# A list schedule with one key per operation in place of a table by operation names

## The chip, the cores and the metric

The kernel runs on one core of one Trainium2 chip. The metric is the device time of one execution in microseconds (us). Five engines work side by side, each on its own list of instructions, in the order in which the program was built: PE (TensorE, matmuls), DVE (VectorE), ACT (ScalarE), POOL (GpSimd) and SP (SyncE, which here only issues DMAs). An instruction that needs something from another engine waits for a semaphore, and everything behind it on its engine waits as well.

## The reference

Two batches of 2048 tokens with 512 features go through a Mamba-2 layer and a feed-forward layer with ternary weights; each is added to its input and normalised. Cut to what is computed:

```python
def reference(u, W_in, conv_w, conv_b, dt_bias, A_log, D, norm_w, W_out, W_up, W_gate, W_down):
    # mamba: 1024 inner features, 8 heads of 128, state of 64, one group
    zxbcdt = einsum('bld,ed->ble', u, W_in)
    z, xBC, dt = zxbcdt[..., :1024], zxbcdt[..., 1024:2176], softplus(zxbcdt[..., -8:] + dt_bias)
    xBC = silu(conv_b + sum(shifted(xBC, k) * conv_w[:, k] for k in range(4)))   # causal, 4 taps
    x, B, C = xBC[..., :1024], xBC[..., 1024:1088], xBC[..., 1088:]
    y = ssd(x, dt, -exp(A_log), B, C) + x * D        # scan over time, in chunks
    yg = y * silu(z)
    yn = yg * rsqrt(mean(yg * yg) + 1e-5) * norm_w
    x1 = layernorm(u + einsum('ble,de->bld', yn, W_out))
    # feed-forward: 2048 hidden features, weights rounded to -1, 0, 1 times mean(|W|)
    up, gate = einsum(x1, ternary(W_up)), einsum(x1, ternary(W_gate))
    return layernorm(x1 + einsum(silu(up) * gate, ternary(W_down)))
```

## The kernel before

**Operations and planner.** The kernel doesn't call the engines in the order of its text. It first records operations: `op(name, engine, cost, function, r=..., w=...)` (the method of class `Order`, and its short name `op` in the kernel) notes a name, an engine, a planned duration, what is read and what is written; from the reads and writes come the dependences. There are 5631 operations; one is a few instructions, a group of 8 or 12 matmuls for instance. `run` then plays a list schedule: whenever an engine is free, it takes, of the operations that are ready and find their buffers free, the one with the smallest key. The sequence in which operations are taken is the sequence in which `emit` issues them, so the keys decide the order on every engine, the DMA issues on SP included, and which of the buffers of a pool an operation gets. Buffers in SBUF and PSUM banks are given out by the planner as well.

Two more rules of `run` touch the order: an ACT operation whose function lies in another table than the last one (silu or exp) counts 12 later than its key, and its planned duration grows by 1.3.

**Keys.** `keys` goes through the operations backwards and finds for each the latest start that its due time and its successors allow; then it looks up the operation's name in `TABLE`. A name followed by `@0` is of group 0 or of FFN block 0; a name without it stands for all other groups, whose keys are the table's number plus the group's origin (46 us per mamba group, 765 + 77 us per FFN block). Operations that the table doesn't have keep the latest start, and those without any due time behind them, such as the warm-up groups, get an infinite key: they are taken when nothing else is ready.

**Stages.** The mamba stage works on 16 groups of 256 tokens (two chunks of 128). For a group, by names of operations:

- `ul` loads u, `usq`, `usmm`, `usmx`, `pw`, `rc` find a scale, `uh` (ACT) and `ulo` (DVE) split u into two f16 halves.
- `x0` to `x8` (PE, L633, 12 matmuls of 260 columns each into a bank of "mm"); `t.3` (ACT, L638) and `t.0` to `t.2` (DVE, L640) are the convolution; `xs` is its silu (ACT, L644); `xt` transposes it on PE (L648) into the bank "tr", `xe` copies it out (ACT, L650).
- `z00` to `z12` (PE, L616, 12 matmuls of 344 columns into "mm") and their silu `sz` (ACT, L623).
- `e` to `q7` are the softplus and the step sizes, `cmm` the cumulative sums (PE, L705, L706); they go through DRAM (`cst`, `cr`, `ec`), are subtracted (`sg`, DVE, L724) and go through exp (`xf`, `xg`, `xec`, ACT, L742 to L747).
- For each chunk, `gps`, `yo` (PE, L776, from the state), `st` (PE, L791) and `stu` (DVE, L798, the state's update), `m`, `md` (DVE, L806, L808), `yd` (PE, L813), `yg` (DVE, L815), then the normalisation `ssq`, `rs`, `pw`, `yh` (ACT), `yl` (DVE), two transposing DMAs `th`, `tl`, and `o0` to `o2` (PE, L833, 8 matmuls of 512 columns each into the one bank "po"), copied out by `s` (ACT, L836) and stored by `ss`.

A group's scan is recorded behind the next group's projections, so two or more groups are in work at a time. Beside them run the FFN weights' loads, means and rounding (L857, L877, L878). At the very front 80 groups of 4 matmuls on constants (L572) keep PE busy while the weights come in; they have the bank "po" and no use otherwise.

The FFN stage works on 8 blocks of 512 tokens. Each block is loaded, normalised, split and transposed (`Fs` to `FT`), then goes through 8 pairs: per pair seven products `FP1` to `FP7` (PE, L935, 8 matmuls of 256 columns, a Strassen-like scheme) in banks A, B and C, with copies of half-finished banks in between (`Fk1` to `Fk3`, ACT, L939 and L944: `Fk1` copies A after product 1 into B, and products 6, 7 and 4 go on adding to A), sums on DVE (`Fc`, L940), silu (`Fa`, ACT, L956), and `Fg`, `Fh`, `Fl`. Then 16 downs `Fd` (PE, L1015, 8 matmuls of 512 columns), 4 for each of 4 row tiles, and for each tile the sum `Fr`, the normalisation `Fe`, `Fq`, `Fy`, `Fm` and the store `Fo`.

Of the kernel before, what the change touches and what calls it, by code (L numbers as in the profile page):

```python
# [37 lines left out]
TABLE = {  # L38
    "tl.1@0": -1082.32, "Fl0.7@0": -1029.81, "Fh0.5@0": -1021.38, "Fh1.3@0": -971.19, "xt2@0": -912.02, "gm.0@0":
    -890.46, "x0@0": -869.16, "Fk1.6@0": -867.44, "xs1@0": -839.63, "x3@0": -839.01, "z00@0": -808.27, "Fd12@0":  # L40
    -786.29, "cmm@0": -776.73, "Fq0@0": -760.02, "Fh1.5@0": -752.59, "Fa1.1@0": -742.14, "Fc22.5@0": -740.59,
    "Fc12.7@0": -709.75, "FP5.6@0": -682.02, "Fd10@0": -672.67, "FP6.3@0": -670.8, "Fq3@0": -649.25, "Fc22.7@0":
    -634.31, "Fe1@0": -614.87, "Fa1.3@0": -567.75, "FP6.1@0": -563.53, "md1.1@0": -547.28, "Fd13@0": -524.72, "t33@0":
    -521.47, "FP4.5@0": -514.84, "wb7ld": -512.65, "Fu0@0": -509.75, "Fh0.1@0": -508.71, "wx8rc": -501.51, "FP6.1":
    -500.94, "Fl6@0": -497.1, "Fu1@0": -494.77, "T30": -493.63, "Fh1.4@0": -492.92, "Fp0@0": -490.89, "Fd22@0": -486.86,
    "Fa1.1": -483.51, "FS5@0": -482.63, "t71@0": -479.96, "FP5.7@0": -478.29, "FP2.2@0": -473.05, "md1.1": -463.02,
    "FP4.1@0": -461.9, "t11@0": -460.67, "yl.0@0": -460.49, "Fl0.7": -459.64, "wx3sq": -458.4, "q_5@0": -458.28,
    "Fl1.6@0": -453.42, "Fk2.1@0": -448.32, "ssq.0": -444.97, "Fh0.7@0": -444.58, "xec0@0": -443.77, "t23@0": -443.66,
    "FP6.4@0": -441.24, "Fc22.6@0": -436.89, "T10": -432.63, "Fk3.0@0": -431.18, "q2@0": -429.41, "FP7.3@0": -429.11,
    "FP7.5": -419.45, "s.1@0": -419.15, "Fs3@0": -418.15, "Fk3.4@0": -416.72, "FS4@0": -416.22, "Fk1.2@0": -408.87,  # L50
    "t70@0": -406.53, "q_11@0": -399.23, "FT5@0": -398.13, "FT0@0": -378.4, "wz1hi": -376.4, "Fk2.2@0": -375.97,
    "q_9@0": -375.64, "t72@0": -373.53, "wb0hi": -371.27, "cst0": -370.61, "t11": -370.46, "xe2@0": -370.3, "Fl0@0":
    -369.99, "t82@0": -366.39, "szs1": -362.42, "q_3@0": -361.43, "Fl1.7@0": -360.58, "Fa2.7@0": -358.67, "t12@0":
    -356.74, "q3@0": -354.24, "Fk3.6@0": -350.89, "th.0@0": -350.43, "Fk1.5@0": -344.81, "stc.0@0": -344.79, "FT4@0":
    -341.61, "xe": -340.43, "Fl0.4@0": -339.88, "nA0": -339.38, "xw0.0@0": -335.61, "Fg0.0@0": -334.33, "usq@0":
    -330.91, "xt3@0": -330.1, "t42@0": -329.77, "Fg1.3@0": -329.03, "Fs2@0": -327.97, "wz2lo": -327.63, "FP1.1@0":
    -324.63, "xf": -321.24, "FP5.6": -321.23, "Fk1.2": -319.88, "FP7.1@0": -319.05, "rs.0@0": -318.4, "xt4": -317.17,
    "m1.0@0": -315.45, "t63": -314.69, "Fc22.4@0": -314.08, "Fh0.6@0": -313.89, "Fm1@0": -312.11, "Fa1.5@0": -309.81,
    "Fr3@0": -307.28, "FP3.1": -306.64, "Fq1@0": -296.16, "xe4@0": -296.16, "Fk2.0@0": -294.21, "Fu2@0": -291.89, "t40":
    -291.26, "cs0@0": -289.33, "Fr1@0": -288.39, "cwu1": -288.17, "cst@0": -283.89, "yd1.0@0": -283.77, "Fl0.0@0":  # L60
    -282.86, "FP3.6@0": -282.73, "FP3.1@0": -282.02, "xt0@0": -281.89, "wz1mm": -281.66, "Fg1.4@0": -280.5, "FT1@0":
    -279.98, "Fa1.4@0": -279.57, "yg1.1@0": -279.25, "wz0mm": -277.61, "Fl1.4@0": -276.92, "ul@0": -276.33, "t21@0":
    -276.31, "Fo3@0": -275.9, "cr1@0": -274.67, "Fy1@0": -272.88, "v0@0": -272.69, "Fr1": -271.9, "x5@0": -271.5,
    "Fh1@0": -270.66, "md0.0": -270.5, "Fg1.7@0": -270.05, "Fa2.0@0": -269.63, "cwu2": -269.24, "ulo@0": -268.86, "q6":
    -266.76, "FP1.7@0": -266.69, "Fk2.6@0": -266.34, "FP6.5@0": -265.81, "Fl1.0@0": -262.07, "Fe2@0": -261.65, "xs5@0":
    -260.73, "t51@0": -259.32, "Fk3.0": -259.28, "q1@0": -257.63, "z12@0": -257.38, "w.1@0": -256.22, "z02": -256.2,
    "t00@0": -255.05, "Fd01@0": -252.69, "Fk2.3": -252.63, "Fk2.3@0": -252.59, "wz1sq": -250.67, "t41@0": -245.47,
    "Fl1.1@0": -244.44, "t53@0": -244.39, "FP6.2@0": -244.14, "xe6@0": -243.32, "wz2ld": -242.79, "yd0.0@0": -242.71,
    "yg1.0@0": -241.61, "Fk2.4@0": -241.29, "xt4@0": -240.8, "o0.1": -240.31, "usmm@0": -239.74, "Fa1.5": -239.11,
    "uh@0": -237.96, "Fh3@0": -237.49, "dec.1@0": -236.73, "x1@0": -236.47, "t10@0": -236.24, "T23": -234.51, "Fg0.2@0":  # L70
    -234.41, "Fk2.1": -233.45, "wa0sq": -232.87, "Fe1": -232.63, "FP2.0@0": -231.31, "sz01@0": -231.12, "cum@0":
    -230.52, "Fl1.5@0": -227.7, "Fd23@0": -224.82, "FP3.4@0": -219.76, "wa3ld": -218.65, "t83": -217.47, "wz2mm":
    -217.46, "wx8lo": -214.51, "s.1": -214.04, "B221": -213.03, "Fe0@0": -211.73, "t73@0": -211.18, "Fk1.4@0": -211.14,
    "cmm": -210.95, "FP2.0": -209.78, "sg10@0": -208.66, "wz1mx": -205.49, "ss.0": -205.18, "pw.1@0": -204.83, "Fd03":
    -204.67, "Fk1.5": -204.52, "cwu8": -204.49, "Fa1.0": -203.81, "Fq0": -202.95, "xs7@0": -202.94, "usrc@0": -202.76,
    "Fa1.6": -202.63, "FT0": -201.78, "cr0": -201.74, "wz2sq": -201.52, "wz1lo": -201.5, "wb1ld": -201.22, "q_13@0":
    -200.82, "t10": -200.74, "x4": -200.25, "Fh0.3@0": -199.89, "ss.0@0": -198.48, "m1.0": -198.16, "Fr2@0": -197.86,
    "t12": -197.66, "tl.1": -197.64, "pw.0@0": -197.63, "Fb0@0": -197.35, "Fk3.7@0": -196.78, "z11@0": -196.42,
    "Fg0.5@0": -196.41, "t03@0": -196.28, "FP7.6": -195.93, "Fy3@0": -194.44, "Fa0@0": -193.51, "Fc22.4": -192.44,
    "Fa1.0@0": -192.03, "Fc22.7": -191.85, "Fk2.2": -190.18, "FP1.6@0": -189.35, "t61": -187.48, "yg1.1": -187.45,  # L80
    "gm.0": -187.19, "q1": -187.08, "xw1.0": -187.03, "xe5": -185.91, "wa1ld": -185.85, "sz11@0": -182.63, "xs1":
    -180.96, "Fd11": -179.42, "w.0@0": -179.3, "wa6sq": -179.25, "cr0@0": -179.11, "FP7.3": -178.62, "ssq.0@0": -177.36,
    "t81@0": -177.35, "xw1.0@0": -177.3, "T13": -177.18, "yg0.0@0": -176.27, "FP1.1": -175.5, "T15": -175.02, "ce.0":
    -174.62, "Fm1": -174.48, "b120": -174.16, "FP5.5": -173.76, "FP1.7": -172.98, "sz10": -172.86, "Fq2@0": -172.61,
    "Fk2.5@0": -171.75, "sg01@0": -171.72, "t20@0": -171.69, "ec0@0": -171.34, "Fq3": -171.06, "gps.0@0": -170.97,
    "xt7@0": -169.8, "FP2.1@0": -166.65, "Fl0.2@0": -166.03, "xt0": -165.84, "m1.1@0": -164.73, "t82": -164.45,
    "FP2.7@0": -163.73, "v0": -161.32, "xf@0": -160.29, "Fa1.2": -157.69, "Fd12": -157.51, "Fl1.4": -156.86, "rl@0":
    -155.76, "Fl1.2@0": -155.13, "wa4ld": -155.01, "Fh0.5": -154.58, "t71": -154.48, "Fa1.6@0": -154.18, "uh": -153.14,
    "FP3.3": -153.11, "t32": -151.43, "s.0@0": -151.17, "Fk3.6": -150.11, "Fr2": -149.91, "Fk1.7@0": -149.48, "FP2.6@0":
    -148.96, "Fd11@0": -148.44, "w.0": -144.84, "Fk1.1@0": -144.72, "wa5ld": -144.27, "Fl0.3": -142.48, "yl.0": -139.87,  # L90
    "xe3@0": -139.73, "wx3ld": -139.56, "m0.1@0": -138.24, "q_7@0": -136.65, "wb4hi": -136.39, "o0.0@0": -135.93,
    "yd0.0": -134.31, "FP7.6@0": -134.12, "e": -133.35, "Fg1.1@0": -133.22, "Fd21@0": -132.86, "Fl0.3@0": -132.74,
    "xt5@0": -132.67, "Fh0.2@0": -130.28, "xe7@0": -129.95, "cwu0": -129.65, "Fk2.4": -128.59, "Fh1.3": -128.55,
    "wz2pw": -127.77, "Fc12.5@0": -127.62, "Fd13": -127.6, "v1": -126.64, "Fh1.6@0": -126.14, "Fl1@0": -126.02, "xe@0":
    -125.7, "FP7.4@0": -125.31, "FT2@0": -125.04, "Fh2@0": -124.79, "v1@0": -124.68, "Fg0.3@0": -124.54, "Fh0@0":
    -124.44, "Fc12.4@0": -124.27, "t40@0": -123.09, "t32@0": -122.64, "sz12": -122.54, "xs2@0": -121.89, "wa7sq":
    -121.13, "sg11@0": -121.02, "t52@0": -120.81, "Fl0.1@0": -120.46, "Fg1.5@0": -120.2, "Fg1.6": -120.08, "Fg0.2":
    -119.75, "Fa2.4@0": -119.35, "Fl5@0": -118.64, "wb3lo": -116.11, "cwx8": -113.29, "Fl0.6@0": -113.23, "Fa2@0":
# [980 lines left out]
```

## Time and profile before

| what | value |
|---|---|
| median of three runs | 1395.8 us (1394.88 to 1397.48) |
| the profiled execution's own time | 1392.94 us |
| its span, from the first to the last instruction | 1391.2 us |
| busy PE, DVE, ACT, POOL | 1374.3, 1083.2, 901.8, 80.9 us |
| matmuls | 10278 |
| moved by DMA | 147.03 MB, mean 106 GB/s |
| busy PE from 0 to 400, 400 to 700, 700 to 790 us | 394.71, 296.94, 88.55 us |
| tables loaded on ACT, one | 1.283 us |

Busy time is the union of an engine's instructions; a matmul's record reaches beyond the start of the next one, since matmuls are pipelined. A line such as `PE mm L616 <- ACT sz L623: 1.6, 4, 0.6` reads: matmuls of line 616 waited for ACT instructions of line 623, 1.6 us in total, 4 times, 0.6 us at most. PEld are the weight loads of PE; they run beside its matmuls.

### The profile page before, as it was taken

What the parts mean: (1) busy time and instruction counts of PE and PEld (TensorE: products, weight loads), DVE (VectorE), ACT (ScalarE), POOL (GpSimd) and SP (SyncE); (2) the same over time, 40 slices, a digit from 0 to 9 for tenths busy, and PEclk for the clock granted to TensorE, in tenths of its full rate; (3) what the DMA queues carried; (4) which work ended last, traced back from release to release, by engine and by line L of the source; (5) the groups of instructions that cost most, each with busy time, mean ns of one, the idle gap of its engine ahead of it and who ended that gap; (6) DMA issues with size and microseconds to landing.
All of it is one profiled execution on the core that took longest, in us unless ns stands there. A gap on an engine that the chain in (4) does not pass through costs nothing.

```text
span 1391.2 us, 26837 instructions
## 1 busy us (share of the span) xinstructions
PE 1374.3 (99%) x10278; PEld 986.6 (71%) x10278; DVE 1083.2 (78%) x2839; ACT 901.8 (65%) x1605; POOL 80.9 (6%) x128
## 2 busy tenths in 40 slices
PE   9999999999999999999999999999999999999997
PEld 8777667666776767766766776768677777767683
DVE  4898889978888999998999755848575775848473
ACT  7888887878768665756677654646455564636461
POOL 1001000000000000000000000000000000000000
PEclk9999999999999999999999999999999999999999
DMA  5354455543444565366558322222222222221100
GB/s 200 113 168 139 118 162 145 166 116 92 129 138 130 119 164 142 98 157 156 141 124 226 114 39 76 55 61 70 58 86 56 76 54 84 54 76 39 46 8 31
DMA packets 186256, 147.03 MB, mean 106 GB/s; under 512 B 133904, under 2 KB 142352, under 8 KB 185872
## 3 DMA queue, kind: packets, MB, share of 16 engines
q1 hardware_dynamic: 186128, 145.33, 39.1%
q8 instruction: 80, 1.31, 0.4%
q14 instruction: 48, 0.39, 0.1%
HBM read 90.63 MB, written 23.20 MB: 82 GB/s over the span
## 4 chain that ended last, share of the span: by engine, by line
PE 69%; DVE 14%; ACT 10%; DMA 4%; issue 2%; POOL 0%; SPq 0%; POOLq 0%; ACTq 0%; DVEq 0%
PE sd L935 18%; PE mm L935 8%; PE ms L1015 8%; PE po L1015 8%; PE mm L616 7%; PE mm L633 6%; PE po L833 6%; DVE acc L640 4%; PE tr L935 2%; PE sd L813 2%; DVE cr L724 1%; PE sd L776 1%; DVE y L815 1%; PE tr L648 1%; DVE yl L825 1%
## 5 line engine op out<-in xcount | busy, mean ns | idle before, releaser
L640 DVE SCALAR_TENSOR_TENSOR acc<-mm,cwu,acc 128x256 f32<-128x256 f32 x432 | 201.6, 476 | 16.4 <-ACT acc L638 14.3
L633 PEld LDWEIGHTS <-wx 128*128 128x128 f16 x1728 | 164.5, 97 | 39.5 <-DVE acc L640 4.1
L633 PE MATMUL mm<-uh,wx 128*128 128x260 f16 x1152 | 152.5, 274 | 2.1 <-DVE acc L640 1.4
L616 PE MATMUL mm<-wz,uh 128*128 128x344 f16 x768 | 127.7, 309 | 1.9 <-ACT sz L623 1.6
L833 PE MATMUL po<-wo,th 128*128 128x512 f16 x512 | 121.0, 379 | 1.4 <-DMA th<-yh 0.8
L961 ACT ACTIVATE sz<-y 128x512 f16<-128x512 f32 x128 | 79.1, 626 | 56.7 <-DVE y L960 54.6
L935 PEld LDWEIGHTS <-xt 128*128 128x128 f16 x1024 | 100.2, 98 | 21.0
L935 PEld LDWEIGHTS <-wx 128*128 128x128 f16 x1024 | 100.2, 98 | 19.1
L935 PEld LDWEIGHTS <-wz 128*128 128x128 f16 x1024 | 100.1, 98 | 15.1
L638 ACT ACTIVATE acc<-mm,cst,cwu 128x256 f32<-128x256 f32 x144 | 79.5, 556 | 41.7 <-PE mm L633 41.3
L616 PEld LDWEIGHTS <-uh 128*128 128x128 f16 x768 | 73.9, 98 | 40.0 <-issue 3.4
L962 DVE TENSOR_TENSOR cr<-y,sz 128x512 f16<-128x512 f32 x128 | 86.3, 686 | 15.5 <-ACT sz L961 14.3
L1015 PE MATMUL ms<-wo,sz 128*128 128x512 f16 x256 | 97.0, 379 | 0.0
L1015 PE MATMUL ms<-wo,cr 128*128 128x512 f16 x256 | 97.0, 379 | 0.0
L1015 PE MATMUL po<-wo,sz 128*128 128x512 f16 x256 | 97.0, 379 | 0.0
L1015 PE MATMUL po<-wo,cr 128*128 128x512 f16 x256 | 97.0, 379 | 0.0
L633 PE MATMUL mm<-ul,wx 128*128 128x260 f16 x576 | 87.5, 273 | 0.0
L833 PEld LDWEIGHTS <-th 128*128 128x128 f16 x512 | 48.9, 98 | 53.5 <-issue 4.0
L1015 PEld LDWEIGHTS <-sz 128*128 128x128 f16 x512 | 50.1, 98 | 50.0
L1015 PEld LDWEIGHTS <-cr 128*128 128x128 f16 x512 | 50.1, 98 | 50.0
L623 ACT ACTIVATE sz<-mm,szs 128x344 f32<-128x344 f32 (+1 forms) x96 | 51.8, 539 | 37.3 <-PE mm L616 33.8
L935 PE MATMUL sd<-fraw,wx 128*128 128x256 f16 x576 | 73.8, 273 | 0.0
(206 smaller groups left out, 2875.4 us busy)
## 6 DMA issues: line engine op xcount, KB each, us to landing
cr<-cum_scratch SPq DMA_DIRECT2D x32, 512.0 KB, 4.9
uraw<-in_uT_dram SPq DMA_DIRECT2D x16, 520.0 KB, 4.4
ec<-cum_scratch SPq DMA_DIRECT2D x64, 128.0 KB, 4.9
fraw<-in_wupT_dram SPq DMA_DIRECT2D x32, 256.0 KB, 2.9
s_scratch<-s SPq DMA_DIRECT2D x32, 256.0 KB, 2.3
x<-s_scratch SPq DMA_DIRECT2D x32, 256.0 KB, 2.9
fraw<-in_wgateT_dram SPq DMA_DIRECT2D x32, 256.0 KB, 3.2
fraw<-in_wdownT_dram SPq DMA_DIRECT2D x32, 256.0 KB, 3.5
```

What stands on the lines that cost most here:

```text
L616: T.matmul(ps[:, :ZC], (uh, ul)[a][:, k, HL + c * P:HL + (c + 1) * P], wz4[b]()[:, j, k, :], start=(n == 0), stop=(n == 11))
L623: op(f"sz{c}{j}", "S", act(w, 1), lambda: S.activation(d["sz"][c][:, j * ZC:j * ZC + w], ps[:, :w], AF.Silu, scale=szs[:, j:j + 1]), r=[ps ...
L633: T.matmul(ps[:, :TW], wx4[a]()[:, j, k, :], (uh, ul)[b][:, k, :], start=(n == 0), stop=(n == 11))
L638: op(f"t{j}3", "S", act(TG, 2), lambda: S.activation(acc.ap, ps[:, HL:TW], AF.Identity, bias=cb[:, j:j + 1], scale=cwu[:, j, 3:4]), r=[ps, ...
L640: op(f"t{j}{k}", "V", stt(TG), lambda k=k: V.scalar_tensor_tensor(acc.ap, ps[:, 1 + k:1 + k + TG], cwu[:, j, k:k + 1], acc.ap, ALU.mult, A ...
L648: T.transpose(tr[:, c * P:(c + 1) * P], xc[:, c * P:(c + 1) * P], ident)
L813: T.matmul(yp[hf][:, i * P:(i + 1) * P], cr[:, h, :], xt[:, c, h, :], start=is_first(g, c), stop=(is_first(g, c) or i == 3))
L833: T.matmul(po.ap, t[:, k, :], wo3[b]()[:, k, :], start=(q == 0 and k == 0), stop=(q == 2 and k == 7))
L935: T.matmul(bank_[:, fi * TG:(fi + 1) * TG], wt[:, kt, f * P:(f + 1) * P], xT[i][:, a, :, kt, :], start=(first and fi == 0 and n == 0), sto ...
L961: o(f"h{t}", "S", 0.54, lambda g_=g_, hv=hv, hh_=hh_: S.activation(hv(hh_), two(g_), AF.Copy), r=[g_], w=[(hh_[p // 2], (p, t))])
L962: o(f"l{t}", "V", tt(512), lambda g_=g_, hv=hv, hh_=hh_, hl_=hl_: V.tensor_tensor(hv(hl_), two(g_), hv(hh_), ALU.subtract), r=[g_, (hh_[p ...
L1015: T.matmul(po.ap, h[qd][:, f, c * P:(c + 1) * P], wd[qd // 2][:, 4 * (qd % 2) + f, :], start=(qd == 0 and f == 0 and a == 0), stop=(qd == ...
```

## The change

Only `keys` and its table differ. The table by names is gone; in its place stands one number for each of the 5631 operations, in the order in which they are recorded, in tenths of a us of the planner's time. The computation of the latest starts is gone as well, since no operation is left without a number: the 80 warm-up groups have one too. The numbers were found by passes through the program backwards and forwards. `run`, the costs, the buffers and the operations themselves are the same.

```diff
-TABLE = {
-    "tl.1@0": -1082.32, "Fl0.7@0": -1029.81, "Fh0.5@0": -1021.38, "Fh1.3@0": -971.19, "xt2@0": -912.02, "gm.0@0":
...
-}
+KEYS = """
+21 40 90 104 116 118 126 128 146 218 252 262 280 305 312 314 322 198 292 335 362 396 398 417 419 431 165 208 220 241
...
+13744 13762 13773 13780 13782 13790
+"""
...
     def keys(self):
-        for o in reversed(self.ops):
-            end = float("inf") if o.due is None else o.due
-            for s in o.succ:
-                end = min(end, s.ls)
-            o.ls = end - o.cost - o.lat - o.kb * 1.024 / self.BW
-        for o in self.ops:
-            t = TABLE.get(f"{o.nm}@{o.g}", TABLE.get(o.nm))
-            o.key = o.ls if t is None else o.org + t
+        for o, k in zip(self.ops, KEYS.split(), strict=True):
+            o.key = int(k) / 10
```

In the built programs the same instructions stand in another order on every engine. Three places by example. SP's list began with a 256 KB piece of W_out and the constants ahead of the first u; now the first u is at its head. In the FFN stage the order on PE was nearly the same in each block; now each block has its own. The downs of one block stand among the products of the next in both programs, before in its first half, now up to its last pairs. ACT's list, with 76 table loads before, has 54.

## The prediction

> **What bounds the kernel now.** I read the page's busy shares first, then busy time by stretches, then the waits of PE (TensorE), last the groups and the time line.
>
> ```profile
> PE 1374.3 (99%) x10278; PEld 986.6 (71%) x10278; DVE 1083.2 (78%) x2839; ACT 901.8 (65%) x1605; POOL 80.9 (6%) x128
> PE   9999999999999999999999999999999999999997
> DVE  4898889978888999998999755848575775848473
> ACT  7888887878768665756677654646455564636461
> ```
>
> PE is busy in every slice but the last; DVE is full only in the first half, ACT never. The stretches separate the mamba stage (to about 780 us), the FFN stage and the tail:
>
> ```profile
> 0.00:100.00 100.00, 97.34 (x791) 76.73 (x792) 74.72 (x236) 83.48 (x151) 9.94 (x21) 1.00 0.52 165
> ...
> 400.00:500.00 100.00, 99.51 (x750) 71.29 (x748) 94.16 (x284) 67.15 (x122) 5.43 (x8) 1.00 0.46 125
> 500.00:600.00 100.00, 99.31 (x727) 68.65 (x725) 94.41 (x285) 63.89 (x119) 4.89 (x7) 1.00 0.58 153
> 600.00:700.00 100.00, 98.12 (x725) 68.03 (x724) 94.03 (x280) 63.73 (x119) 4.13 (x6) 1.00 0.57 137
> ...
> 790.00:1384.00 594.00, 594.00 (x4439) 434.01 (x4437) 387.73 (x719) 318.07 (x530) 33.70 (x54) 1.00 0.22 56
> 1384.00:1391.20 7.20, 0.14 (x1) 0.00 (x0) 2.31 (x8) 1.62 (x2) 1.10 (x2) 0.72 0.20 74
> ```
>
> Columns: stretch, its length, busy PE, PEld, DVE, ACT, POOL, granted clock, DMA. From 790 to 1384 us PE has no idle time at all: 594.00 of 594.00, at clock 1.00. So the FFN stage can't be shortened by another order, only lengthened. PE's idle time is 1391.2 - 1374.3 = 16.9 us; 7.1 of it is the tail behind the last matmul (7.20 - 0.14), 1.1 the wait for the first constants at the start. That leaves 16.9 - 7.1 - 1.1 = 8.7 us, spread over the mamba stage. The waits of PE name them:
>
> ```profile
> PE mm L616 <- ACT sz L623: 1.6, 4, 0.6
> PE mm L633 <- DVE acc L640: 1.4, 4, 0.4
> PE tr L648 <- ACT xt L650: 1.2, 2, 0.7
> PE po L572 <- DVE ones L418: 1.1, 1, 1.1
> PE tr L648 <- ACT xc L644: 1.0, 2, 0.8
> PE po L833 <- DMA th<-yh: 0.8, 1, 0.8
> PE po L833 <- ACT s L836: 0.6, 2, 0.3
> PE mm L633 <- ACT acc L638: 0.4, 1, 0.4
> PE sd L813 <- ACT yh L823: 0.3, 1, 0.3
> PE sd L776 <- DVE state L794: 0.3, 1, 0.3
> PE mm L633 <- ACT sz L623: 0.2, 1, 0.2
> ```
>
> Without the constants they add up to 7.8 us in 19 waits; the other 0.9 us is gaps that the profile puts down to nobody. No wait is long: each is a matmul that stood a little too early behind its producer. That is what an order can mend, and nothing else here.
>
> Is a PE that is 99% busy really full? The time line of the last downs says so:
>
> ```profile
> 1377.29 0.38 PE L1015 MATMUL ms<-wo,cr 128*128 128x512 f16 x1
> 1377.50 0.38 PE L1015 MATMUL ms<-wo,sz 128*128 128x512 f16 x1
> ```
>
> Each lasts 0.38 us but the next starts 0.21 us later, and so it goes on for the whole stage. A rule speaks against me here: the Trainium skill, Perfetto Trace Analysis, Identifying the Most-Contended Engine, says that matmul busy time is a bad measure of headroom and the share of weight loads a good one. By it, 71% would leave 1391.2 x 0.29 = 400 us to win (an estimate by that page). The steady spacing of 0.21 us decides against it, since no reordering changes that.
>
> **The change part by part.** No matmul, vector operation or DMA is added or removed: the two built programs hold the same ones, 10278 matmuls among them. What moves is the order on every engine. From the built orders I take positions only, and weigh PE's by start-to-start intervals of the trace of before (a z group of 12 matmuls 1.75 us, an x group 1.345, an o or a down group of 8 1.727, an FFN product 0.873, a pair of transposes 0.245, yd 0.894, st 1.016, yo 1.094).
>
> 1. Distance on PE between a producer's matmuls and the matmuls that need what comes of them, shortest and median, before to after: x to its transposes 3.70 and 8.65 to 4.29 and 11.91 us; yd.1 to o0, which has the normalisation and the transposing DMA between, 8.22 and 11.53 to 10.85 and 20.73; st to the next chunk's yo, with the state update between, 0.55 and 2.54 to 2.00 and 9.87; reuse of the mm banks 0.25 and 4.21 to 1.09 and 4.31; reuse of the po bank 1.02 and 3.71 to 1.59 and 4.64. These pairs are the waits above, but one: reuse of the tr bank, 0.87 and 4.19 to 0.87 and 3.58, gets no better. So I keep its 1.2 us and, since nothing tells what they are, the 0.9 us of unnamed gaps less a little, 0.8; together 2.0. Gain: 8.7 - 2.0 = 6.7 us. Bounds: 8.7 if all goes; nothing if each wait only meets another queue.
>
> 2. Distances that shrink. The scale sum of u to the next x8, shortest 12.78 to 5.86 us: between stand 0.15 (DVE), 0.60 (POOL), 0.15 (DVE), 1.15 (ACT) and 1.29 (DVE), 3.3 us by the groups of before, so 2.5 us remain as cover. The cumulative sums (cmm) to the next yd0.0, shortest 29.51 to 24.81: in the trace cmm at 393.2, the copy at 394.1, the first row product L724 at 400.9 after two DMAs, then 4 x 0.8 of these, a table load 1.28, an exp of 1.04 (L743), 4 x 0.263 and 0.6 on DVE, in all about 15 us. Cover 10 us. Both cost nothing; if DVE is late by more than that cover, PE stops once in each of 16 groups.
>
> 3. ACT loads tables less often: 76 loads in the built program before, 54 after. One of before's groups:
>
> ```profile
> L644 ACT ACT_TABLE_LOAD x25 | 32.1, 1283 | 1.4 <-DVE acc L640 1.0
> ```
>
> 22 x 1.283 = 28.2 us of ACT's 901.8. ACT is off the path, so I book it at nothing; it makes the ACT waits of PE (1.6 + 1.2 + 1.0 + 0.6 + 0.4 + 0.3 + 0.2 = 5.3 us of the list) less likely. The skill's page ScalarE: Activation LUTs, What ACT_TABLE_LOAD costs, adds a drain of 1.38 us to each load; no row here shows it, and by it ACT would win 22 x 2.66 = 58.5 us (an estimate), still nothing on the path.
>
> 4. Changes between f16 and f32 matmuls on PE: 404 to 412. The start-to-start time of a z group is 1.746 us at least and 1.843 at its 90th percentile, which I take as the price of a badly placed neighbour, 0.1 us: 8 x 0.1 = 0.8 us more. Bounds 0 and 1.6.
>
> 5. The loads at the front: SP began with a piece of W_out and the small constants ahead of u; now u is first. The 80 warm groups (0.436 us each, 34.9 us) fill PE until the weights are there, in both, and all of them run in both: nothing. If they ran out, each us that a weight comes late would be a us of PE; the last stands behind 68.6 us of PE work before, behind 77.2 after.
>
> 6. The tail: the last four downs, their sums and stores are the same sequence, Fr, Fe, Fq, Fy, Fm and Fo of the last rows: nothing. FFN products and downs of two blocks are now mixed differently in each block; shortest distance from a product to the one that needs its copied bank 1.73 us before and after: nothing, as long as ACT copies at once.
>
> Sum: -6.7 + 0.8 = -5.9 us. On the profiled execution (1392.94, span 1391.2) that makes 1387.0. The three runs had a median of 1395.8, 2.9 above the profiled one, so the forecast is 1395.8 - 5.9 = 1389.9, 0.42% less.
>
> **The rivals.** First, DVE takes over: it is busy 94% between 400 and 700 us. For: with PE's waits gone the same DVE work must fit into less time, and a queue that is 94% full has 3 x 5.8 = 17 us left over 300. Against: of the 8.7 us only 0.49 + 0.69 + 1.88 = 3.1 lie in that stretch, 5.6 outside, and DVE's head start is hardly smaller: PE work that stands ahead of a group, less the DVE work up to what the group needs, was at least 68 us between 500 and 600 us of PE work and is 65. Then the 3.1 us stay lost, and 5.6 - 2.0 - 0.8 = 2.8 are won: 1393.0; with all of it given back 1395.8. Second, more than the idle time is won: taking for each pair of neighbouring kinds on PE the lower-quartile spacing, PE's list adds up to 1360.3 us against 1381.1 measured from first to last group, so 20.8 us is the most an order can win; a third beyond the 8.7 would make 1395.8 - 8.7 - 4.0 = 1383.1. Nothing in the trace names that time, so it is unlikely. Third, slower: the FFN stage loses its even beat. There a copy of a bank takes 0.58 us (L944) and is done about 0.95 us after the last product is issued, against a distance of 1.73: 0.78 us of cover. For: ACT is 54% busy there (318.07 of 594.00) and one silu of 0.69 with one cast of 0.63 standing ahead of the copy uses the cover up. 64 pairs, so from a mean loss of 5.9 / 64 = 0.09 us per pair the gain is gone, and with 0.2 us it is 12.8 us: 1389.9 + 12.8 = 1402.7. Against: the shortest distance is that of before, which had not one wait there, and from product to down the shortest grew from 3.49 to 4.35, the median from 18.24 to 34.03. That the order isn't changed at all is excluded by the built programs.
>
> **How the numbers follow.** Forecast 0.70, DVE 0.16, more won 0.05, FFN slower 0.09. Measurement can't tell less than about 0.2%, 2.8 us, from no change. Faster by more (under 1393.0): 0.70 + 0.05 and a third of the DVE case, 0.80; slower by more: most of the FFN case, 0.08; within: 0.12. The range goes from full gain less the scatter of the runs, 1395.8 - 8.7 - 2.6 = 1384.5, to just under no change, 1395.5, which takes in most of the DVE case.
>
> **What would show it.** PE's idle time between 1.1 us and the last matmul down from 8.7 to about 2 us; 790 to 1384 still without idle time; ACT busy about 870 us; 54 table loads; the tail 7 us. I am wrong if PE waits for L944 or L939 in the FFN stage, if DVE is named in most of PE's waits, or if idle time is gone and the span isn't shorter.

## The result and the profile after

Four runs of the changed kernel had a median of 1389.8 us (1387.61 to 1390.52), four of the kernel before 1396.47 (1394.88 to 1397.48): a ratio of 0.9954, interval 0.9941 to 0.9966, 0.46% or 6.7 us less. The forecast was 1389.9. A second measurement of the same changed kernel, five runs beside 23 of before, gave 0.9954 again (0.9941 to 0.9967). The profiled execution took 1387.61 us with a span of 1385.9, against 1391.2 before.

The page's busy shares and three lines of slices, after:

```profile
PE 1370.4 (99%) x10278; PEld 986.3 (71%) x10278; DVE 1075.2 (78%) x2839; ACT 871.4 (63%) x1583; POOL 89.2 (6%) x128
...
PE   9999999999999999999999999999999999999998
DVE  5698889987889999998999764939576665849363
ACT  7778767786768765675666563737465554737441
```

PE is full up to the tail and DVE in the first half, much as before. The instruction counts of PE, DVE and POOL are those of before. ACT has 22 fewer, 1583 for 1605, and 30.4 us less busy time, 22 x 1.283 = 28.2 of it table loads. Two of their groups (line, operation, number, busy time, mean ns of one, idle time ahead):

```profile
L830 ACT ACT_TABLE_LOAD x16 | 20.5, 1283 | 0.5 <-DMA cr<-cum_scratch 0.3
L732 ACT ACT_TABLE_LOAD x14 | 18.0, 1283 | 0.2
```

Lines are 88 further down than before, so L732 is the silu of x, where before had 25 loads. The stretches (length, then busy PE, PEld, DVE, ACT, POOL, granted clock, DMA):

```profile
400.00:500.00 100.00, 100.00 (x737) 69.71 (x734) 94.40 (x294) 68.30 (x122) 4.36 (x7) 1.00 0.52 146
500.00:600.00 100.00, 98.35 (x761) 71.21 (x761) 93.30 (x273) 65.85 (x124) 4.35 (x6) 1.00 0.50 132
600.00:700.00 100.00, 98.27 (x718) 67.18 (x713) 93.81 (x283) 64.06 (x117) 6.37 (x8) 1.00 0.56 144
790.00:1377.00 587.00, 587.00 (x4387) 429.02 (x4386) 376.10 (x709) 311.82 (x524) 38.78 (x54) 1.00 0.24 57
1377.00:1385.90 8.90, 2.08 (x10) 0.77 (x8) 3.76 (x10) 1.63 (x2) 1.09 (x2) 0.90 0.16 60
```

The FFN stage is still without any idle time, and the tail behind the last matmul is 8.90 - 2.08 = 6.8 us (7.1 before). But PE's idle time is 1385.9 - 1370.4 = 15.5 us; less that tail and 1.1 at the start, 7.6 remain, where 8.7 stood before. The span is 5.3 us shorter and visible idle time fell by 1.1 and 0.3 alone; the other 3.9 us went out of "busy" PE (1374.3 to 1370.4), with the same 10278 matmuls at the same clock. And PE's waits name another engine:

```profile
PE mm L704 <- DVE acc L728: 2.5, 3, 1.2
PE mm L721 <- DVE acc L728: 2.0, 3, 1.4
PE mm L704 <- ACT sz L711: 1.5, 3, 0.6
PE po L660 <- DVE half L512: 1.1, 1, 1.1
PE sd L1031 <- DVE y L903: 0.4, 1, 0.4
PE mm L721 <- DVE v L709: 0.3, 1, 0.3
PE ms L582 <- ACT wx L596: 0.2, 1, 0.2
PE tr L736 <- ACT xc L732: 0.2, 1, 0.2
PE mm L721 <- ACT sz L711: 0.2, 1, 0.2
```

Without the constants (L660), DVE has 5.2 of 7.3 us, mostly in six waits for a bank that the convolution (L728) still reads. Before, ACT had 5.3 of 7.8. One of the six on the time line (start, duration, engine, line, operation, tiles; in brackets the idle time ahead and what ended it):

```profile
598.24 1.66 DVE L812 TENSOR_SCALAR cr<-cr,cum 128x128 f32<-128x128 f32 x8 [1.25 <-DMA cr<-cum_scratch]
...
599.58 1.08 PE L879 MATMUL sd<-xw,bt 128*64 128x256 f32 x8
...
601.34 0.47 DVE L728 SCALAR_TENSOR_TENSOR acc<-mm,cwu,acc 128x256 f32<-128x256 f32 x1
...
601.87 0.32 PE L704 MATMUL mm<-wz,uh 128*128 128x344 f16 x1 [1.21 <-DVE acc L728]
```

The row products (L812) stand first in DVE's queue and wait 1.25 us for a DMA. The convolution behind them, which needs no DMA, frees its bank late, and PE stops for 1.21 us with DVE as the engine named.

**How much busy time hides a stop.** The last row holds it: that z matmul has a record of 0.32 us, while 12 of them start within 1.75 us, 0.146 apart. So a record reaches about 0.17 us past the next matmul's start, as with the downs shown before (0.38 long, 0.21 apart). Where PE stands still, up to 0.17 us of it lies under the last record and counts as busy; only the rest shows as idle. A stop must therefore be counted from start to start. I took each run of consecutive matmuls of one line, tile and shape as a group, the time from its start to the next group's start, and, as the undisturbed time, the shortest tenth of groups of that line, shape and number. An excess of 0.13 us or more is a stop:

| profile | span | stops | their time | span less stops | of it 400 to 700 us |
|---|---|---|---|---|---|
| before | 1391.2 | 48 | 15.8 | 1375.4 | 18, 6.1 us |
| before, again | 1392.8 | 50 | 16.6 | 1376.2 | 16, 5.9 us |
| changed | 1385.9 | 28 | 11.7 | 1374.2 | 11, 5.0 us |
| changed, again | 1388.9 | 27 | 14.0 | 1374.9 | 12, 6.1 us |

About 20 stops went, those of the short kind: under 0.3 us there were about 30 in either profile of before, now 14 and 9. 20 to 23 stops at 0.17 us are 3.4 to 3.9 us, the busy time that fell (3.9 in the first pair; 1375.5 to 1371.0, 4.5 us, in the second, where visible idle time even rose by 0.9). What is left of the span without stops differs by 1.2 and 1.3 us, 0.3 of it the tail. The stops thus explain 4.2 of 5.3 and 2.6 of 3.9 us; the remaining us, beyond the tail, lies in no stop of this size and stays unexplained. They also say where: 400 to 700 us gave 1.1 in the one pair and -0.2 in the other, the rest of the kernel 3.1 and 2.8.

### The profile page after: what moved, and what is told of

It reads as the page before. It is cut to its first block, busy times and chain, and to the rows that moved or that the text cites. A ratio compares the mean times of both kernels' runs of the same rounds, so it can differ in the third digit from the quotient of the medians.

```text
span 1385.9 us, 26844 instructions
## 1 busy us (share of the span) xinstructions
PE 1370.4 (99%) x10278; PEld 986.3 (71%) x10278; DVE 1075.2 (78%) x2839; ACT 871.4 (63%) x1583; POOL 89.2 (6%) x128
## 4 chain that ended last, share of the span: by engine, by line
PE 76%; DVE 14%; ACT 4%; DMA 4%; issue 1%; SPq 0%; POOL 0%; POOLq 0%; DVEq 0%; ACTq 0%
PE sd L1023 18%; PE mm L721 9%; PE mm L1023 8%; PE po L1103 8%; PE ms L1103 8%; PE mm L704 8%; PE po L921 7%; DVE acc L728 3%; PE sd L901 3%; PE tr L1023 2%; DVE cr L894 1%; PE tr L736 1%; PE sd L879 1%; PE sd L864 1%; DVE cr L812 1%
## 5 line engine op out<-in xcount | busy, mean ns | idle before, releaser
L728 DVE SCALAR_TENSOR_TENSOR acc<-mm,cwu,acc 128x256 f32<-128x256 f32 x432 | 201.5, 478 | 18.3 <-ACT acc L726 16.1
L726 ACT ACTIVATE acc<-mm,cst,cwu 128x256 f32<-128x256 f32 x144 | 80.2, 557 | 56.9 <-PE mm L721 56.5
L1049 ACT ACTIVATE sz<-y 128x512 f16<-128x512 f32 x128 | 78.3, 625 | 29.6 <-DVE y L1048 23.0
L732 ACT ACTIVATE xc<-acc 128x256 f32<-128x256 f32 x128 | 52.5, 413 | 43.4 <-DVE acc L728 42.8
```

The lines of the kernel that those rows point to most:

```text
L726: op(f"t{j}3", "S", act(TG, 2), lambda: S.activation(acc.ap, ps[:, HL:TW], AF.Identity, bias=cb[:, j:j + 1], scale=cwu[:, j, 3:4]), r=[ps, ...
L728: op(f"t{j}{k}", "V", stt(TG), lambda k=k: V.scalar_tensor_tensor(acc.ap, ps[:, 1 + k:1 + k + TG], cwu[:, j, k:k + 1], acc.ap, ALU.mult, A ...
L732: op(f"xs{j}", "S", silu(TG), lambda: S.activation(xc.ap, acc.ap, AF.Silu), r=[acc], w=[xc], table="silu")
L1049: o(f"h{t}", "S", 0.54, lambda g_=g_, hv=hv, hh_=hh_: S.activation(hv(hh_), two(g_), AF.Copy), r=[g_], w=[(hh_[p // 2], (p, t))])
```

## The experiments

Two theories stood against each other. By the first (A in the quoted expectations) the gain comes of the distances on PE's list between a producer and its user. By the second (B there) it comes of ACT, which has 22 table loads less in its queue. Ratios are to the kernel before; "against the changed kernel" is the difference of the ratios times 1395.5 us.

**More work on ACT.** In 27 of the 48 magnitude passes of the weights, ACT does the operation twice more, 54 passes in all; the order is that of the changed kernel. The expectation takes 0.52 us for each. In the trace they took 0.626, and ACT's busy time rose by 33.4 us (871.4 to 904.8), somewhat more than the 28.2 of the 22 loads.

```diff
+            def mag(n=n, i=i, q=q, raw=raw):
+                for _ in range(2 if n % 16 < 9 else 0):
+                    S.activation(raw.ap, raw.ap, AF.Abs)
+                S.activation(raw.ap, raw.ap, AF.Abs, accum_out=sums[:, i, q:q + 1])
...
```

> The order after, with 27 of the 48 magnitude operations of the FFN weights (ACT, L945) doing their absolute value twice more: 54 instructions of about 0.52 us, 28 us more work on ACT, as much as the 22 saved table loads. Theory A (the gain comes from matmuls that no longer stand too close behind their producers): ACT has room, at most 1.5 us above the changed kernel, ratio to before 0.995 to 0.9965. Rival B (the gain is ACT's saved table loads): the gain is given back, ratio 0.999 or more.

Measured: 1409.81 us, 1.0106 (1.0091 to 1.0121), 21.2 us more than the changed kernel: 0.63 us for each us of ACT. The gain is given back, as B has it, and 15 us more, which neither theory had. PE's waits in its profile:

```profile
PE mm L704 <- DVE acc L728: 5.6, 7, 1.6
PE tr L736 <- ACT xt L738: 5.2, 6, 2.6
PE mm L704 <- ACT sz L711: 3.8, 3, 2.9
PE mm L721 <- DVE acc L728: 3.5, 5, 1.4
```

ACT's own waits come back (5.2 and 3.8 us), and DVE's double, though DVE got no work. What DVE itself waits for, in the changed kernel and here, says why (the convolution's first step, L726, is ACT's):

```profile
DVE acc L728 <- ACT acc L726: 16.1, 22, 3.4
```

```profile
DVE acc L728 <- ACT acc L726: 29.7, 29, 3.4
```

DVE waits for ACT, and PE for DVE. So ACT, 63% busy, is not off the path in the sense of step 3. Two caveats. These passes come in lumps of over a us in places that no planner knew. And not all of the 21.2 us is waiting: from 100 to 200 us the granted clock was 0.97 in this profile (1.00 in the changed kernel), which is at most 3 us (100 x 0.03).

```profile
100.00:200.00 100.00, 92.20 (x663) 63.39 (x662) 79.26 (x244) 79.75 (x164) 6.87 (x9) 0.97 0.48 133
```

**The same in small lumps.** In the same 27 places one pass over 256 columns. The expectation takes 0.28 us each, 7.6 in all; in the trace it was 0.41 us each, 11.0 in all.

```diff
+                if n % 16 < 9:
+                    S.activation(raw[:, :256], raw[:, :256], AF.Abs)
...
```

> The order after, with the same 27 places on ACT delayed by 0.28 us instead of 1.04 (7.6 us in all). If ACT's time passes to PE in proportion, as 21 of 28 us did: 5.7 us, ratio 0.9995. If each place has cover of some tenths of a us (theory A, distances on PE are longer now): under 2 us, ratio 0.997 or less.

Measured: 1392.92 us, 0.9976 (0.9965 to 0.9986), 3.1 us more, 0.28 per us of ACT: between the two expectations, less than in lumps, still far from nothing. What grows most is again DVE's part:

```profile
PE mm L704 <- DVE acc L728: 5.9, 6, 1.5
PE mm L721 <- DVE acc L728: 4.1, 6, 1.4
```

**One distance undone.** The keys of the 128 transposes xt come 20 us of the planner's time earlier (not 10 tenths, as the expectation's "lowered by 10" reads), so that their distance to x falls from 4.29 at least and 11.9 in the median to 3.55 and 6.6; 56 loads instead of 54. The numbers are a hundred times as large as in the changed kernel, those of xt 20000 smaller besides. The planner plays the whole list again, so other operations move as well: about a fifth of DVE's and of ACT's stand in another order than in the changed kernel.

```diff
-21 40 90 104 116 118 126 128 146 218 252 262 ...
+2100 4000 9000 10400 11600 11800 12600 12800 14600 21800 25200 26200 ...
...
-            o.key = int(k) / 10
+            o.key = int(k) / 1000
```

> The order after, but the keys of the transposes xt lowered by 10, so that they follow their x groups closely again: distance on PE shortest 3.55 and median 6.6 us (after 4.29 and 11.9, before 3.70 and 8.65); 56 table loads. Theory A: waits of the transposes for ACT and DVE come back, 1 to 4 us above the changed kernel, ratio 0.996 to 0.9985. Rival B: hardly a table load more, so no change, 0.995.

Measured: 1393.03 us, 0.9985 (0.9977 to 0.9994), 4.3 us of the gain gone, with two loads more (2.6 us of ACT, which at even 0.63 would be 1.6 us). That the distances count, as A has it, rests less on this time, in which the other moves have a part, than on the waits. In the profile (lines are another 105 further down) ACT's silu is again what the transposes wait for, six times:

```profile
PE tr L841 <- ACT xc L837: 2.9, 6, 0.8
PE mm L826 <- DVE acc L833: 2.0, 3, 1.4
PE mm L809 <- DVE acc L833: 1.2, 2, 1.0
```

**No table loads, in either order.** Every exp of the mamba stage becomes a copy, so the kernel leaves out the decays and the softplus; two table loads are left of 76. First in the kernel before:

```diff
-            op("xf", "S", 0.95, lambda: S.activation(d["cr"][0].ap, d["cr"][0].ap, AF.Exp), ...
+            op("xf", "S", 0.95, lambda: S.activation(d["cr"][0].ap, d["cr"][0].ap, AF.Copy, scale=0.001), ...
...
-                op("xe", "S", 0.12, lambda: S.activation(e.ap, e.ap, AF.Exp, scale=-1.0), ...
+                op("xe", "S", 0.12, lambda: S.activation(e.ap, e.ap, AF.Copy, scale=-0.001), ...
```

> The kernel before, its order unchanged, with a scaled copy in place of every exp (the decays and the softplus are not computed), so that ACT loads no tables: 76 x 1.283 = 97 us less on ACT. Rival B (the table loads make PE wait): at least as much as the change won, ratio 0.9965 or less. Theory A (matmuls stand too close behind producers on all engines): the waits for DVE and DMA stay, less than 3 us won, ratio 0.998 or more.

Measured: 1388.78 us, 0.9952 (0.9938 to 0.9966), 6.7 us less than before, the whole size of the change, with the old order. Its page:

```profile
PE 1372.5 (99%) x10278; PEld 987.5 (71%) x10278; DVE 1083.0 (78%) x2839; ACT 810.1 (58%) x1531; POOL 80.8 (6%) x128
```

ACT is 91.7 us less busy, so each us is worth only 0.07. But B's mechanism is there: PE's waits put down to ACT fall from 5.3 to 2.9 us (L650 1.2, L623 1.0, L638 0.4, L823 0.3), those put down to DVE don't (1.7 to 2.0). The same edit in the changed kernel:

> The changed kernel in the same way: 54 x 1.283 = 69 us less on ACT. Theory A: ACT's waits are only 1.9 of the 7.6 us that PE stands idle, ratio to before 0.993 to 0.9955. Rival B: it ends where e5 ends, so the order itself is worth less than 1 us.

Measured: 1385.46 us, 0.9930 (0.9915 to 0.9946), 3.3 us less than the changed kernel. Set side by side, in us against before:

| | old order | new order | difference |
|---|---|---|---|
| with table loads | 0 | -6.4 | 6.4 |
| without | -6.7 | -9.8 | 3.1 |

With the loads gone the new order still wins 3.1 us (about 2.9 either way, from the two intervals): that part is the order without loads, in which the distances are the most likely reason. The other 3.3 (about 3.2 either way) need the loads to be there, and they are not simply the worth of 22 loads: 74 loads less gave 6.7 us in the old order, 0.09 each, 52 less gave 3.3 in the new, 0.06 each. At the old price the 22 would be 2.0 us (an estimate from these runs); the rest would be that the new order bears its 54 better. So loads and distances both have a part, and these intervals don't say how large. What still stops PE without loads is DVE:

```profile
PE mm L721 <- DVE acc L728: 2.8, 4, 1.4
PE mm L704 <- DVE acc L728: 2.4, 3, 1.3
```

**Half of the loads, in the old order.** Only the exps of the second chunk's decays and of the state's decays become copies: 38 loads for 76.

```diff
-            op("xg", "S", 0.95, lambda: S.activation(d["cr"][1].ap, d["cr"][1].ap, AF.Exp), ...
+            op("xg", "S", 0.95, lambda: S.activation(d["cr"][1].ap, d["cr"][1].ap, AF.Copy, scale=0.001), ...
...
-                op(f"xec{c}", "S", act(512), lambda c=c: S.activation(d["ec"][c].ap, d["ec"][c].ap, AF.Exp), ...
+                op(f"xec{c}", "S", act(512), lambda c=c: S.activation(d["ec"][c].ap, d["ec"][c].ap, AF.Copy, scale=0.001), ...
```

> The kernel before, order unchanged, with scaled copies in place of the exps of the second chunk's decays and of the state's decays only: 38 table loads instead of 76, 48.8 us less on ACT. If the loads cost PE time in proportion (6.7 us for 76): 3.3 us less, ratio 0.9976. If only the first few matter or the exps' results themselves: nearly all of 6.7, 0.9955, or nothing, 1.000.

Measured: 1393.51 us, 0.9988 (0.9979 to 0.9996), 1.7 us less. 38 loads of 76 would be 3.3 us by count. The run's interval (0.6 to 2.9) leaves that out, but the 6.7 has one of its own (4.7 to 8.7), half of which is 2.4 to 4.3, so the two overlap. That a load's price depends on where it stands is suggested here and not shown.

**The loads put back.** In groups 1 to 11 of the changed kernel, a one-column exp ahead of the last copy of the transposes makes ACT load the exp table and then the other again: 22 loads more, 76 in all.

```diff
+                    def xcopy():
+                        if j == 3 and 1 <= g <= 11:
+                            S.activation(mhalf[:, 2:3], mhalf[:, 3:4], AF.Exp)
...
```

> The changed kernel with 22 table loads put back: in groups 1 to 11 a one-column exp ahead of the copy xe3, which makes ACT load the exp table and then the silu table again, 76 loads as before, nothing else moved. Theory D (half of the gain is the saved loads, half the order of the rest): 2 to 5 us above the changed kernel, ratio to before 0.997 to 0.999. Theory A alone (loads without part in it): under 1 us, below 0.996.

Measured: 1397.8 us, 1.0014 (1.0006 to 1.0023), 8.4 us more than the changed kernel: the whole gain and 2 us on top, more than either theory had. Its page and waits:

```profile
PE 1372.3 (98%) x10278; PEld 986.1 (71%) x10278; DVE 1073.0 (77%) x2839; ACT 901.0 (65%) x1616; POOL 89.4 (6%) x128
```

```profile
PE mm L704 <- DVE acc L728: 5.9, 7, 1.2
PE mm L721 <- DVE acc L728: 3.6, 6, 1.4
PE mm L721 <- DVE v L709: 1.6, 3, 1.2
PE tr L736 <- ACT xt L741: 1.4, 3, 0.8
```

ACT's busy time is that of before (901.0 to 901.8), and the time is 0.14% above it. Yet of the four longest waits only one, of 1.4 us, is put down to ACT; the others show as DVE's. A caveat: these loads stand where no plan expected them, and in the first two runs work added in such places cost 0.28 and 0.63 us per us (here 8.4 for 29.6), so 8.4 us is not the price of before's 22.

**Fewer warm-up groups.** 64 instead of 80, 16 x 0.437 = 7.0 us of PE without use. The planner plays the shorter list again, and about a quarter of DVE's operations come to stand in another order.

```diff
-WARM = 80
+WARM = 64
```

> The order after without 16 of the 80 warm-up groups: 16 x 0.437 = 7.0 us less work on PE. Rival C (PE's list is the bound from the first matmul on): 7.0 us less than the changed kernel, ratio 0.990. Theory A (the front waits for weights and for ACT and DVE, the warm-up only fills): PE's idle time in the first 100 us grows by about 6 us and the time stays within 2 us, ratio 0.994 to 0.997.

Measured: 1385.39 us, 0.9932 (0.9920 to 0.9944), 3.1 us less than the changed kernel, between the two expectations. The first 100 us in the changed kernel and in this one:

```profile
0.00:100.00 100.00, 96.86 (x806) 78.80 (x807) 70.49 (x229) 75.79 (x140) 9.09 (x20) 1.00 0.41 132
```

```profile
0.00:100.00 100.00, 92.13 (x756) 73.69 (x757) 73.13 (x233) 79.34 (x145) 11.53 (x20) 1.00 0.45 146
```

4.7 us of the 7.0 come back as idle time right there, so the warm groups stood for the most part where PE would have waited anyway; the other moves may have a share in it. Step 5 held that all of them run in both kernels at no difference, which stands.

**The planner's own numbers.** The list is played with durations that the planner holds for each operation. Some differ from the spacings in the trace; here they are set to these, and the keys are sought anew by the same kind of passes with small random shifts. Once with 64, once with 80 warm groups.

```diff
-            o("gps", "PE", 0.45, ...
+            o("gps", "PE", 0.38, ...
...
-                o("yo", "PE", 1.3, ...
+                o("yo", "PE", 1.094, ...
...
-                o("st", "PE", 1.25, ...
+                o("st", "PE", 1.05, ...
...
-        op("wasc", "V", 2.5, ...
+        op("wasc", "V", 1.41, ...
...
-            o.key = int(k) / 10
+            o.key = int(k) / 1000
```

> The changed kernel with the planner's durations of PE's operations set to the spacings that the trace shows (they add up to about 1361 us instead of 1372), 64 warm-up groups, and keys sought again for these. Theory A': the waits left in the changed kernel come from PE running ahead of a plan with too long PE durations, so they shrink: ratio 0.988 to 0.992, 4 to 9 us under the changed kernel, PE's waits named by the profile under 4 us. If what is left is chance in DMA and semaphore times, nothing is won: ratio 0.994 to 0.997.

Measured: 1383.45 us, 0.9919 (0.9904 to 0.9934), 4.9 us less than the changed kernel, as A' has it, with a part of the warm groups in it. But PE's named waits did not shrink to under 4 us: without the constants they add up to 6.4, against 7.3 in the changed kernel.

> As the refitted kernel, but with all 80 warm-up groups. If measured PE durations in the plan are worth 2 us and the 16 warm-up groups 3: ratio 0.994. If the refit alone is worth all: 0.992.

Measured: 1381.99 us, 0.9900 (0.9886 to 0.9914): 14 us less than before and 7.5 less than the changed kernel, the best of all and better than either expectation. With a fitted plan taking warm groups away brings nothing that shows (0.9919 against 0.9900, the intervals overlap). Page and waits of the one with 80:

```profile
PE 1367.9 (99%) x10278; PEld 986.1 (71%) x10278; DVE 1074.5 (78%) x2839; ACT 876.1 (63%) x1585; POOL 87.4 (6%) x128
```

```profile
PE mm L827 <- DVE sc L689: 1.6, 2, 1.3
PE po L766 <- DVE half L618: 1.1, 1, 1.1
PE mm L827 <- DVE acc L834: 1.0, 1, 1.0
PE mm L827 <- ACT sz L817: 0.7, 1, 0.7
PE mm L810 <- DVE acc L834: 0.5, 1, 0.5
```

ACT does as much as in the changed kernel (876.1 to 871.4, two loads more), and the waits for the convolution fall from 4.5 to 1.5 us; the longest left is put down to the scale of u (L689). So a third order, with ACT's work held, brought about as much again as the change. Whether the fitted durations did it isn't shown: the keys were sought anew as well, in finer steps and with random shifts, and no run sought them anew with the old durations.

**Both kernels once more,** unchanged, beside the rest.

> The changed kernel itself, on the same chip as the two others: 0.994 to 0.9965.

> The kernel before against itself: how far two series of the same program stand apart, ratio 0.999 to 1.001, and a second profile of it. If PE's idle time is what makes the time, an execution of about 1395.5 us has 2 to 3 us more of it than the first profile's 8.7.

Measured: 0.9954 (0.9941 to 0.9967) and 0.9998 (0.9989 to 1.0007). A difference of 0.1% can't be told from none here. The second profile of before has a span 1.6 us longer than the first, but only 0.4 us more visible idle time (9.1 for 8.7) and 1.2 us more busy PE, so the expectation that idle time makes the time isn't borne out. Their profiles are the second pair of the table of stops; the same count for the other runs:

| profile | span | stops | their time | span less stops |
|---|---|---|---|---|
| ACT more, lumps | 1408.1 | 49 | 34.1 | 1374.0 |
| ACT more, small | 1393.1 | 35 | 19.0 | 1374.1 |
| xt sooner | 1390.6 | 34 | 14.7 | 1375.9 |
| before, no loads | 1386.2 | 38 | 11.4 | 1374.8 |
| before, 38 loads | 1390.1 | 43 | 15.4 | 1374.7 |
| changed, no loads | 1383.2 | 17 | 8.7 | 1374.5 |
| changed, loads back | 1396.5 | 40 | 22.6 | 1373.9 |
| fitted, 80 warm | 1380.7 | 18 | 7.3 | 1373.3 |
| changed, 64 warm | 1383.1 | 35 | 15.5 | 1367.6 |
| fitted, 64 warm | 1379.0 | 25 | 10.4 | 1368.6 |

The spans of all kernels with 80 warm groups lie 27 us apart (1380.7 to 1408.1), their spans less stops within 1373.3 to 1376.2, and some 7 us lower with 64. Whatever an edit did on ACT or DVE, it reached the end through stops of PE and little else. (For the first row, matmuls at the lower clock are in the count of stops.)

## Why the prediction was right, and where not

The time was right (1389.9 forecast, 1389.8 measured), the cause half right, and the sum right by luck: step 1 measured its gain by the wrong thing, step 3 left a gain out, and the two made up for each other.

**What bounds it:** right. PE's list sets the end, and stops on it are nearly all that an order changes; the FFN stage stayed full (587.00 of 587.00).

**Step 1, distances:** right in kind. Bringing the transposes close again cost 4.3 us, with other moves beside it, and brought back six waits of theirs; without the table loads the new order is still 3.1 us faster, hardly more than its interval. But its size was read from the wrong measure: visible idle time was to fall from 8.7 to 2.0 us and fell to 7.6, in the second pair it rose from 9.1 (1392.8 - 1375.5 - 7.1 - 1.1) to 10.0 (1388.9 - 1371.0 - 6.8 - 1.1). The term of 6.7 us did not happen as I put it: most waits of before went, the 1.2 us that I kept among them (the one for the silu of z stayed, 1.6 and 1.5 us), but others, nearly all of them DVE's, came in their place (7.8 us named before, 7.3 after). It came right in the sum since 20 short stops went whose time is for the most part inside PE's busy time.

**Step 2, shrunk distances at nothing:** as put for cmm; no wait for it appears. For DVE behind it the time line shows what was not costed: the row products now wait for their DMA at the head of DVE's queue and hold the convolution up.

**Step 3 failed:** "ACT is off the path, so I book it at nothing." Its sizes were right (54 loads, ACT busy 871.4 for about 870), its booking not. Without loads the kernel before is 6.7 us faster, with 22 put back in other places the changed one is 8.4 slower, and 33.4 us of other ACT work cost 21.2. Of the gain of 6.4 us about 3.3 hang on the loads being there, give or take as much. The cause of the error: I read ACT's share of busy time. My own list put 5.3 of 7.8 us of PE's waits down to ACT, and step 1 took all of them for a matter of distance alone; an ACT that is done sooner ends them too. And where work was added to ACT, much of its delay reached PE by way of DVE, under whose name it stands. That "nothing else" than an order can mend these waits was wrong for the same reason.

**Step 4, f16 and f32 neighbours:** +0.8 us predicted, and it did not happen as put. Of the changes between f16 and f32 matmuls, 69 of 403 before and 85 of 411 after have a spacing that is longer by 0.07 to 0.13 us, 6.3 and 7.8 us in all. But so have 83 and 59 spacings between different operations of one type, 7.5 and 5.2 us. Together that is 13.8 and 13.0 us, no more than before: the 0.1 us is real, but most changes of type don't have it, and as many other changes do.

**Step 5, the front, and step 6, tail and FFN:** nothing, as put; the tail gave 0.3 us.

**Rivals.** DVE taking over was right in its place and its sign: DVE is named in 5.2 of 7.3 us of PE's waits, which I had called the mark of being wrong, and 400 to 700 us gave 1.1 and -0.2 us. It was wrong in what that is worth: it allowed 2.8 us in all, and 6.4 to 6.7 were measured. And some of DVE's name covers others: DVE waited for a DMA in the stop shown above, and for ACT in the runs with more work there. The FFN rival fell: not one stop there. "More won" is not borne out for this change, but the kernel with the fitted plan shows that it was there: 14 us under before, of 20.8 that the spacings allowed at most.

**Open:** how much of the gain is loads and how much distances; which single loads matter; whether the fitted durations or the new search won the 7.5 us. The old order with 22 of its own loads less was not run. Orders put together from the old one up to some time and the new one behind it were not tried.

## What to carry to other kernels

Measure a full engine's stops from start to start of its instructions, not as idle time: where records overlap, short stops hide in the busy share. An engine that is 63% busy in an order fixed beforehand is not free: follow its delay through the engine that waits for it before booking a change on it at nothing. And before seeking a better order, it is worth setting the planner's durations to the spacings of the trace: here that, together with a new search, brought as much again as the change.

## What the runs showed that I had not expected

- Work added where the plan doesn't know of it costs 0.28 to 0.63 us per us of ACT (8.4 of 29.6, 3.1 of 11.0, 21.2 of 33.4), work taken away gives 0.07 (6.7 of 91.7). In all of these every queue kept the order that was made for the old times, a likely reason that no run tests.
- A table load costs its 1.283 us and hardly more: the median gap to its neighbours on ACT is 17 ns ahead and 11 ns behind, over 75 loads of the trace before. The Trainium skill, ScalarE: Activation LUTs, What ACT_TABLE_LOAD costs, adds 1.38 us of drain, which no run here shows.
- Taking useless matmuls off a full engine gives only a part of their time back: with 16 of 80 warm groups less, 4.7 of 7.0 us came back as idle time in the first 100 us, and 3.1 were won.
